# Layer 0's queries of ten token tiles as pairs in seven quadrant products each, with token sums and weight forms made by GpSimd

## The chip, the cores and the metric

The kernel runs on one core of a Trainium2 chip. The metric is device time in microseconds (us) of one execution; the kernel before takes 1817.35 us, the median of three runs (1817.26 to 1817.72). PE is TensorE's matmuls, PEld its weight loads, DVE is VectorE, ACT is ScalarE, POOL is GpSimd, SP is SyncE, which here only issues transfers.

## The reference

Two layers of a graph transformer on 2708 tokens with 512 features, 8 heads of 64, all in float32. Each token attends only to its neighbours (and itself), some 9 on average. Cut to one layer:

```python
mask = adj.astype(jnp.float32) + jnp.eye(n)
q = (h @ Wq.T + bq).reshape(n, 8, 64)
k = (h @ Wk.T + bk).reshape(n, 8, 64)
v = (h @ Wv.T + bv).reshape(n, 8, 64)
scores = jnp.einsum('nhd,mhd->hnm', q, k) / jnp.sqrt(jnp.float32(64))
attn = softmax(jnp.where(mask[None] == 0, -1e9, scores))
ctx = jnp.einsum('hnm,mhd->nhd', attn, v).reshape(n, 512)
h1 = layer_norm(h + ctx @ Wo.T + bo, ln1_g, ln1_b)
ff = relu(h1 @ W1.T + b1) @ W2.T + b2
h2 = layer_norm(h1 + ff, ln2_g, ln2_b)
```

## The kernel before

A token tile is 128 tokens; there are 22 (`NT`), the last of 20 tokens. Layer 0 is run in three stages.

**The keys' pass** (function `first`): for each tile `t`, PE makes its keys and values from the transposed tokens `xg` (four 128x512 matmuls each, L626 in `project`), ACT copies both out of PSUM (L962, L968), POOL adds the keys' bias (L964), and ACT's queue writes the rows to `kv_d`. Tokens are held in three buffers of two tiles each. Beside it, `lists_of` turns the adjacency matrix into lists of neighbours: ACT codes a row block (L746), DVE takes the largest entries (L751 to L758). After the last list, DVE counts (`counted`, L772 to L824: `has`, `count`, `hot`, the running sum `before` and its prefix `run`, L789 to L813), and PE ranks the tokens by their number of neighbours (`ranked`, L834 and L841, matmuls that read `hot` and `before`). These four matmuls stand in PE's queue ahead of the last tile's keys and values (L621) and of every query.

**The queries' pass** (`first_queries`): per tile four 128x512 matmuls against `Wq` (L626), then one DVE instruction that scales, adds the bias and writes to SBUF (`evicted`, L1003). Pairs of tiles are written to `q_d`. After the third tile's product, PE turns the ranking round (`inverted`, L900, 22 small matmuls), DVE makes two index tables of it (L909 to L913), and then `last_keys` (L989 and six times L636) adds up the last tile's keys and values, which it takes from the PSUM places in which they have lain since the keys' pass; their write to `kv_d` is what the first gathers of attention wait for. Between the query tiles stand three "own" queries (L1077) and, from the eighth tile on, steps of attention.

**The blocks**: attention (gathers on POOL's queue, DVE and ACT arithmetic) runs beside out projection and feed forward of eleven blocks of two tiles. From the fifth block on the second feed-forward matrix is multiplied in seven products per quadrant pair instead of eight (`feed_forward_by_seven`, L1769).

The order on every engine is the order in which the program is written (the kernel schedules by hand); each engine runs its queue in order. PSUM has eight places of 128x512: three in the pool `ps_f` (tag "f"), three in `ps` (tag "g"), and two in `ps_a` (`a0`, `a1`). A place is given out again when its last reader is done. In the order of the tiles, keys take "g" and values "f"; query tiles take "g" and "f" in turn.

## Time and profile before

| | |
|---|---|
| runs | 1817.26, 1817.35, 1817.72 us |
| profiled execution, its own time | 1817.08 us |
| span of that execution on the core | 1815.1 us |
| PE busy | 1791.5 us (99%) |
| DVE busy | 1463.3 us (81%) |
| ACT busy | 1001.1 us (55%) |
| POOL busy | 855.4 us (47%) |
| granted TensorE clock | 0.998 |
| keys' pass, first to last matmul | 5.0 to about 154 us |
| queries' pass | 154.3 to about 250 us |

The profile counts each float32 matmul twice, as two passes: 21 full tiles of queries with four matmuls each stand as 168. A matmul's recorded length (592 ns for 512 columns) overlaps the next one's; what counts is the distance from start to start. Engine time in a stretch is read from the windows' view, the order of events from the timeline, whose columns are start, length, engine, line and operation, what is written and read, shape and count.

### The profile page before, as it was taken

What the parts mean: (1) busy time and instruction counts of PE and PEld (TensorE: products, weight loads), DVE (VectorE), ACT (ScalarE), POOL (GpSimd) and SP (SyncE); (2) the same over time, 40 slices, a digit from 0 to 9 for tenths busy, and PEclk for the clock granted to TensorE, in tenths of its full rate; (3) what the DMA queues carried; (4) which work ended last, traced back from release to release, by engine and by line L of the source; (5) the groups of instructions that cost most, each with busy time, mean ns of one, the idle gap of its engine ahead of it and who ended that gap; (6) DMA issues with size and microseconds to landing.
All of it is one profiled execution on the core that took longest, in us unless ns stands there. A gap on an engine that the chain in (4) does not pass through costs nothing. (4 is left out here: it accounts for less than half of the span.)

```text
span 1815.1 us, 23887 instructions
## 1 busy us (share of the span) xinstructions
PE 1791.5 (99%) x6839; PEld 1214.6 (67%) x6839; DVE 1463.3 (81%) x2599; ACT 1001.1 (55%) x3397; POOL 855.4 (47%) x830
## 2 busy tenths in 40 slices
PE   9999999999999999999999999999999999999997
PEld 4444456666777867777677644666666888788786
DVE  4987778988989889799896267988888899989933
ACT  5771436645555555555653104677776677767631
POOL 3333755534454544454540132556665665655312
PEclk9999999999999999999999999999999999999999
DMA  9997987757676675666752777967867787877531
GB/s 335 369 344 252 374 284 245 230 181 241 203 238 220 203 259 192 208 220 202 241 194 73 242 285 272 319 193 256 279 186 263 243 264 237 293 225 234 173 94 36
DMA packets 186728, 426.74 MB, mean 235 GB/s; under 512 B 20550, under 2 KB 83898, under 8 KB 186584
## 3 DMA queue, kind: packets, MB, share of 16 engines
q0 software_dynamic: 76992, 264.49, 44.0%
q1 hardware_dynamic: 99434, 139.01, 22.5%
q10 hardware_dynamic: 10158, 21.61, 3.1%
q8 instruction: 56, 0.92, 0.2%
q14 instruction: 88, 0.72, 0.1%
HBM read 357.13 MB, written 57.11 MB: 228 GB/s over the span
## 5 line engine op out<-in xcount | busy, mean ns | idle before, releaser
L1119 POOL DMA_INDIRECT kv<-kv_d,listed x420 | 526.0, 1252 | 307.2 <-DVE acc L1195 145.8
L1780 PE MATMUL pf<-hT,w 128*128 128x256 f32 x1792 | 407.2, 379 | 2.1 <-ACT ft L1791 2.1
L1780 PEld LDWEIGHTS pf<-hT,w 128*128 128x128 f32 x1792 | 339.2, 190 | 59.2 <-issue 11.0
L1182 ACT ACTIVATE kv<-kv,p 128x64 f32<-128x64 f32 x1232 | 311.0, 335 | 5.0
L1156 DVE TENSOR_TENSOR kv<-kv,q 128x1024 f32<-128x1024 f32 (+1 forms) x222 | 257.1, 1158 | 14.1 <-DMA q<-q_d,ident_i 10.9
L1162 DVE TENSOR_REDUCE sc<-kv 128x16 f32<-128x1024 f32 (+1 forms) x222 | 258.0, 1162 | 7.6
L1195 DVE TENSOR_TENSOR acc<-acc,kv 128x1024 f32<-128x1024 f32 (+2 forms) x178 | 205.6, 1155 | 49.6 <-ACT kv L1182 36.9
L1596 PEld LDWEIGHTS pf<-hT,w 128*128 128x128 f32 x1024 | 178.5, 190 | 55.3 <-issue 34.6
L1596 PE MATMUL pf<-hT,w 128*128 128x256 f32 (+1 forms) x1024 | 214.6, 357 | 0.1
L1791 ACT ACTIVATE ft<-pf,b 128x256 f32<-128x256 f32 x168 | 78.1, 466 | 214.1 <-PE pf L1780 211.4
L1569 PE MATMUL a<-w,ft 128*128 128x512 f32 x416 | 194.6, 592 | 0.0
L1175 ACT ACTIVATE p<-sc,listed 128x8 f32<-128x8 f32 x420 | 103.6, 295 | 127.9 <-DVE sc L1162 116.5
L1281 POOL TENSOR_TENSOR rd<-va,mhalf 128x1 f32<-128x1 f32 (+1 forms) x48 | 43.8, 913 | 230.8 <-DVE va L1279 230.7
L626 PE MATMUL o<-wo,cT 128*128 128x512 f32 x336 | 151.0, 593 | 0.3 <-ACT cT L1354 0.3
L1188 DVE TENSOR_TENSOR kv<-kv,p 128x512 f32<-128x512 f32 (+1 forms) x178 | 123.6, 694 | 4.8 <-ACT p L1175 4.5
L1569 PEld LDWEIGHTS a<-w,ft 128*128 128x128 f32 x416 | 77.7, 190 | 57.5 <-issue 52.0
L626 PEld LDWEIGHTS o<-wo,cT 128*128 128x128 f32 x336 | 63.4, 190 | 69.3 <-issue 59.6
L1331 POOL TENSOR_SCALAR va<-sq 128x1 f32<-128x1 f32 (+1 forms) x40 | 17.2, 429 | 188.4 <-ACT xb L1324 101.9
L751 DVE MAX8 tops<-code 128x8 f32<-128x247 f32 (+2 forms) x242 | 78.8, 400 | 28.0 <-ACT code L746 27.9
L1226 ACT ACTIVATE cx<-acc,su 128x64 f32<-128x64 f32 (+1 forms) x352 | 88.2, 333 | 11.2 <-DVE su L1218 6.2
L1182 ACT ACTIVATE acc<-kv,p 128x64 f32<-128x64 f32 (+1 forms) x352 | 88.8, 335 | 1.4
L746 ACT ACTIVATE code<-aj 128x1354 bf16<-128x1354 int32 (+1 forms) x44 | 73.5, 1724 | 23.7 <-POOL aj L740 19.0
(258 smaller groups left out, 2793.8 us busy)
## 6 DMA issues: line engine op xcount, KB each, us to landing
forms<-form_d SPq DMA_DIRECT2D x294, 128.0 KB, 3.8
aj<-in_adj SPq DMA_DIRECT2D x42, 677.0 KB, 6.3
kv_d<-kvs ACTq DMA_DIRECT2D x21, 512.0 KB, 7.4
h<-ln_b POOLq DMA_DIRECT2D x41, 256.0 KB, 7.0
xg<-in_xT SPq DMA_DIRECT2D x19, 512.0 KB, 8.0
w<-in_W SPq DMA_DIRECT2D x16, 512.0 KB, 6.4
kv<-kv_d,listed POOLq DMA_INDIRECT x420, 6.5
zT_d<-zT SPq DMA_DIRECT2D x22, 256.0 KB, 5.3
```

Of the source, the lines that this page charges most:

```text
L626: nc.tensor.matmul(o[:r], xs(c), wm[:, c, :], start=(c == 0), stop=(c == NC - 1))
L1119: return nc.gpsimd.indirect_dma_start(out=to, out_offset=None, in_=table[:, :], in_offset=bass.IndirectOffsetOnAxis(ap=s, axis=0), bounds_ ...
L1156: nc.vector.tensor_tensor(kv[:r, :c, :DM], kv[:r, :c, :DM], self.q[:r].unsqueeze(1).to_broadcast([r, c, DM]), ALU.mult,)
L1162: nc.vector.tensor_reduce(self.sc[:r, s0 : s0 + c, :], kv[:r, :c, :DM].rearrange("p s (h d) -> p s h d", d=DK), AX.X, ALU.add,)
L1175: nc.scalar.activation(p[:r, s, :], self.sc[:r, s, :], AF.Exp, bias=minus[:r, g, s : s + 1])
L1182: nc.scalar.activation(to[:, i, hd], kv[:r, i, DM + h * DK : DM + (h + 1) * DK], AF.Copy, scale=p[:r, s0 + i, h : h + 1],)
L1188: nc.vector.tensor_tensor(to[:, 0, :].rearrange("p (h d) -> p h d", d=DK), kv[:r, 0, DM:].rearrange("p (h d) -> p h d", d=DK), p[:r, s0, : ...
L1195: nc.vector.tensor_tensor(self.acc[:r, :c, :], self.acc[:r, :c, :], kv[:r, :c, DM:], ALU.add)
L1226: nc.scalar.activation(cx[:r, hd], self.acc[:r, 0, hd], AF.Copy, scale=self.su[:r, h : h + 1])
L1569: nc.tensor.matmul(a[:r, cols], fts[f][:, c0 : c0 + r], self.w2[f // 2][:, f % 2, cols], start=(f == 0), stop=(f == NFC - 1),)
L1596: nc.tensor.matmul(pf[:, :w], self.w1[f // 2][:, c, f % 2 * P : f % 2 * P + P], hT[:, c, :w], start=(c == 0), stop=(c == NC - 1),)
L1780: nc.tensor.matmul(pf[:, :W], self.w1[j][:, c, f % 2 * P : f % 2 * P + P], hT[:, c, :], start=(c == 0), stop=(c == NC - 1),)
```

## The change

Query tiles 0 to 9 of layer 0 are made as five pairs. A pair is a 256x512 matrix of tokens, `Wq` is 512x512; both are cut into four quadrants, and the product is made of seven quadrant products (Winograd's form) instead of eight. Each quadrant product is two matmuls of 128x256, so a pair has 14 of these in place of 8 of 128x512.

- **Token sums.** For each pair POOL makes four combinations of token quadrants (`token_sums`, 128x256 each) in the keys' pass, after tiles 1, 3, 5, 7 and 9, and keeps them in places of `W1` and `W2` that are free until then.
- **Weight forms.** Four combinations of `Wq`'s quadrants (`formed_of`, 128x512 each) and one difference of the bias's halves (`more`, 128x256) are made by POOL in the keys' pass at tile 19.
- **Scale.** 1/8 is put into `Wq` once, by ACT at tile 18 (128x2048); query evictions no longer scale.
- **Products.** At an even tile four of the seven (`first`), at the odd tile three (`second`). A pair needs four PSUM places: pairs 0, 2, 4 take one "f", one "g", `a0` and `a1`; pairs 1 and 3 take two "f" and two "g".
- **Evictions.** Seven DVE instructions per pair (`begun` five, `ended` two) in place of two.
- **Transfers.** In the second pass over the tokens, the first five `xg` loads leave out a quadrant that no product reads, and come as two transfers. Two pairs of feed-forward weight loads move from query tile 10 to 11 (the first of these places holds weight forms until then).

```diff
--- before.py
+++ after.py
@@ -45,6 +45,8 @@
 LEAD = 1.2
 QT = 16
 OWN = 5
+SUMS = ("w1_2", "w1_3", "w2_3", "w1_4", "w2_4")
+FORMQ = ("w2_2", "w1_1")
 WARM = 7
 LISTS = (4, 7, 9, 12, 13, 14, 15, 17, 18, 19)
 EARLY = 3
@@ -636,6 +638,75 @@
                 nc.vector.tensor_tensor(to, part, to, ALU.add)
             else:
                 nc.vector.scalar_tensor_tensor(to, part, scale, to, ALU.mult, ALU.add)
+
+    W2 = 2 * P
+
+    def formed_of(w, to, by):
+
+        b11, b12, b21, b22 = w[:, :2, :W2], w[:, :2, W2:], w[:, 2:, :W2], w[:, 2:, W2:]
+        t1, t2, t3, t4 = to
+        by.tensor_tensor(t3, b22, b12, ALU.subtract)
+        by.tensor_tensor(t1, b12, b11, ALU.subtract)
+        by.tensor_tensor(t2, b22, t1, ALU.subtract)
+        by.tensor_tensor(t4, b21, t2, ALU.subtract)
+
+    def token_sums(a, b, to, by):
+
+        a11, a12, a21, a22 = a[:, :2, :], a[:, 2:, :], b[:, :2, :], b[:, 2:, :]
+        s1, s2, s3, s4 = to
+        by.tensor_tensor(s1, a21, a22, ALU.add)
+        by.tensor_tensor(s2, s1, a11, ALU.subtract)
+        by.tensor_tensor(s3, a11, a21, ALU.subtract)
+        by.tensor_tensor(s4, a12, s2, ALU.subtract)
+
+    class Seven:
+
+
+        def __init__(self, a, b, sums, w, forms, banks):
+            s1, s2, s3, s4 = sums
+            t1, t2, t3, t4 = forms
+            L, R = slice(0, W2), slice(W2, DM)
+            self.c0, self.c1, self.a0, self.a1 = banks
+            self.first = (
+                (self.c0[:, L], a[:, :2, :], w[:, :2, L]),
+                (self.c0[:, R], s2, t2),
+                (self.c1[:, L], s1, t1),
+                (self.c1[:, R], s3, t3),
+            )
+            self.second = (
+                (self.a0[:, L], a[:, 2:, :], w[:, 2:, L]),
+                (self.a0[:, R], s4, w[:, 2:, R]),
+                (self.a1[:, L], b[:, 2:, :], t4),
+            )
+
+        def products(self, which):
+            for to, left, right in which:
+                for c in range(2):
+                    nc.tensor.matmul(
+                        to, left[:, c, :], right[:, c, :], start=(c == 0), stop=(c == 1)
+                    )
+
+        def begun(self, q, bias, more, wide=None):
+
+            L, R = slice(0, W2), slice(W2, DM)
+            nc.vector.tensor_tensor(q[0], self.c0[:, L], bias[:, L], ALU.add)
+            nc.vector.tensor_tensor(q[3], self.c0[:, R], q[0], ALU.add)
+            nc.vector.tensor_tensor(self.c1[:, L], self.c1[:, L], more, ALU.add)
+            if wide is None:
+                nc.vector.tensor_tensor(q[2], self.c1[:, R], q[3], ALU.add)
+                nc.vector.tensor_tensor(q[1], self.c1[:, L], q[3], ALU.add)
+            else:
+                nc.vector.tensor_tensor(
+                    wide.rearrange("p (two n) -> p two n", two=2),
+                    self.c1.rearrange("p (two n) -> p two n", two=2),
+                    q[3].unsqueeze(1).to_broadcast([P, 2, W2]),
+                    ALU.add,
+                )
+            nc.vector.tensor_tensor(q[3], self.c1[:, L], q[2], ALU.add)
+
+        def ended(self, first, q2):
+            nc.vector.tensor_tensor(first, self.a0, first, ALU.add)
+            nc.vector.tensor_tensor(q2, self.a1[:, :W2], q2, ALU.add)
 
     def finish(steps):
         for _ in steps:
@@ -925,6 +996,12 @@
             t = wts.tile([P, NC, XB], F32, tag=f"w1_{5 + i % 3}", name="xg")
             xg.append(t)
             step = bw if i else P
+            if i >= XBS and i % XBS < len(SUMS):
+                src = chunked(xT)
+                nc.sync.dma_start(out=t[:, :2, :P], in_=src[:, :2, b : b + P])
+                nc.sync.dma_start(out=t[:, 2:, :], in_=src[:, 2:, b : b + bw])
+                yield
+                return
             for a in range(0, bw, step):
                 (by if a else nc.sync).dma_start(
                     out=t[:, :, a : a + step], in_=chunked(xT)[:, :, b + a : b + a + step]
@@ -950,7 +1027,7 @@
         wv = matrix(w, "Wv", "wv")
         pa = tc.tile_pool(name="pa", bufs=2)
         lists, counted, placing = lists_of(pa.__enter__())
-        done, before = 0, None
+        done, before, sums = 0, None, []
         for t in range(NT):
             r = size(t)
             if t == NT - 1:
@@ -980,10 +1057,23 @@
                 bk = row_of(short[0], "bk")
                 nc.gpsimd.tensor_tensor(kv[:r, :DM], kv[:r, :DM], bk[:r], ALU.add)
             meanwhile(t)
+            if t % 2 and t // 2 < len(SUMS):
+                place = wts.tile([P, 4, 2, P], F32, tag=SUMS[t // 2], name="sums")
+                x2 = xg[t // 2]
+                sums.append([place[:, i] for i in range(4)])
+                token_sums(x2[:, :, :P], x2[:, :, P:], sums[-1], nc.gpsimd)
             if t == QT:
                 wq = matrix(w, "Wq", "wq", nc.gpsimd)
+            if t == QT + 2:
+                nc.scalar.activation(wq, wq, AF.Copy, scale=DK**-0.5)
             if t == NT - 4:
                 bq = row_of(short[1], "bq", DK**-0.5)
+            if t == NT - 3:
+                forms = [wts.tile([P, 2, 2, W2], F32, tag=tag, name="forms") for tag in FORMQ]
+                forms = [place[:, i] for place in forms for i in range(2)]
+                formed_of(wq, forms, nc.gpsimd)
+                more = dn.tile([P, W2], F32, tag="hT", name="more", bufs=1)
+                nc.gpsimd.tensor_tensor(more, bq[:, W2:], bq[:, :W2], ALU.subtract)
 
         def last_keys():
             nc.vector.tensor_tensor(kv[:r, :DM], k[:r], bk[:r], ALU.add)
@@ -991,19 +1081,19 @@
             plus_rest(kv[:r, DM:], v, r)
             nc.scalar.dma_start(**before)
 
-        return bq, wq, parts, placing[1], pa, tokens, last_keys
-
-    def first_queries(bq, wq, parts, inverted, pa, tokens, last_keys, meanwhile):
+        sevens = xg, sums, forms, more
+        return bq, wq, sevens, parts, placing[1], pa, tokens, last_keys
+
+    def first_queries(bq, wq, sevens, parts, inverted, pa, tokens, last_keys, meanwhile):
 
         nonlocal at
+        xg, sums, forms, more = sevens
         made = []
 
         def evicted(t, q, qs):
             r = size(t)
-            nc.vector.scalar_tensor_tensor(
-                qs[:r, t % 2], q[:r], DK**-0.5, bq[:r], ALU.mult, ALU.add
-            )
-            plus_rest(qs[:r, t % 2], q, r, DK**-0.5)
+            nc.vector.tensor_tensor(qs[:r, t % 2], q[:r], bq[:r], ALU.add)
+            plus_rest(qs[:r, t % 2], q, r)
 
         def written():
             t, qs = made.pop(0)
@@ -1017,7 +1107,25 @@
 
         for t in range(NT):
             r = size(t)
-            q = project(tokens(t, 1), r, wq, "q", other=t % 2 > 0)
+            xs = tokens(t, 1)
+            seven = t // 2 < len(sums)
+            if not seven:
+                q = project(xs, r, wq, "q", other=t % 2 > 0)
+            elif t % 2 == 0:
+                x2 = xg[t // 2 + XBS]
+                banks = [ps_f.tile([P, DM], F32, tag="f", name="q0")]
+                banks.append(ps.tile([P, DM], F32, tag="g", name="q1"))
+                if t % 4:
+                    banks.append(ps_f.tile([P, DM], F32, tag="f", name="q2"))
+                    banks.append(ps.tile([P, DM], F32, tag="g", name="q3"))
+                else:
+                    banks += [
+                        ps_a.tile([P, DM], F32, tag=f"a{i}", name=f"q{2 + i}") for i in range(2)
+                    ]
+                q = Seven(x2[:, :, :P], x2[:, :, P:], sums[t // 2], wq, forms, banks)
+                q.products(q.first)
+            else:
+                q.products(q.second)
             if t % 2 == 0 and made:
                 written()
             if t == 2:
@@ -1036,7 +1144,15 @@
             if t % 2 == 0:
                 qs = wts.tile([P, 2, DM], F32, tag=f"w2_{5 + (t // 2 + 1) % 3}", name="qs")
                 made.append((t, qs))
-            evicted(t, q, qs)
+            if not seven:
+                evicted(t, q, qs)
+            else:
+                flat = qs.rearrange("p two n -> p (two n)")
+                quarters = [flat[:, i * W2 : (i + 1) * W2] for i in range(4)]
+                if t % 2 == 0:
+                    q.begun(quarters, bq, more, flat[:, W2 : 3 * W2])
+                else:
+                    q.ended(flat[:, :DM], quarters[2])
             if t in LISTS:
                 i = 2 + 2 * LISTS.index(t)
                 for g in order[i : i + 2]:
@@ -1074,8 +1190,8 @@
 
         r = size(g)
         q = project(lambda c: zT[:, c, :r], r, wq, "q")
-        nc.vector.scalar_tensor_tensor(to[:r], q[:r], DK**-0.5, bq[:r], ALU.mult, ALU.add)
-        plus_rest(to[:r], q, r, DK**-0.5)
+        nc.vector.tensor_tensor(to[:r], q[:r], bq[:r], ALU.add)
+        plus_rest(to[:r], q, r)
 
     def put(table, s, rows, group):
 
@@ -1996,9 +2112,9 @@
 
     def beside_queries(t):
 
-        if t in (8, 10, 12, 14):
-            now.load_w1(t // 2 - 4, nc.gpsimd)
-            now.load_w2(t // 2 - 4, nc.gpsimd)
+        if t in (8, 11, 12, 14):
+            now.load_w1(len(now.w1), nc.gpsimd)
+            now.load_w2(len(now.w2), nc.gpsimd)
         if t == 6:
             now.settle()
         if t == 16:
```

Names in the rows below: `q`, with its numbers, is a PSUM place of a query; `forms` and `sums` are the weight forms and token sums; `kvs` are a tile's keys and values on their way to `kv_d`.

On PE, at the head of the queries' pass, the kernel before has:

```order
L834 MATMUL pr<-hot,tri 128x264
L841 MATMUL pr<-before,ones 128x264
L621 MATMUL k<-wk,xg 20x512 x4
L621 MATMUL v<-wv,xg 20x512 x4
L626 MATMUL q<-wq,xg 128x512 x12
```

and the changed one, pair 0 and the first half of pair 1:

```order
L905 MATMUL pr<-hot,tri 128x264
L912 MATMUL pr<-before,ones 128x264
L623 MATMUL k<-wk,xg 20x512 x4
L623 MATMUL v<-wv,xg 20x512 x4
L685 MATMUL q_1269<-wq,xg 128x256 x2
L685 MATMUL q_1269<-forms,sums 128x256 x2
L685 MATMUL q_1270<-forms,sums 128x256 x4
L685 MATMUL q_1271<-wq,xg 128x256 x2
L685 MATMUL q_1271<-wq,sums 128x256 x2
L685 MATMUL q_1272<-forms,xg 128x256 x2
L685 MATMUL q_1298<-wq,xg 128x256 x2
```

Twelve matmuls of 512 columns (three tiles) ahead of L900 have become 22 of 256 columns (a pair and four products of the next). Behind L900 the changed PE goes on with the second half of pair 1 and then pair 2:

```order
L685 MATMUL q_1300<-wq,xg 128x256 x2
L685 MATMUL q_1300<-wq,sums 128x256 x2
L685 MATMUL q_1301<-forms,xg 128x256 x2
L685 MATMUL q_1417<-wq,xg 128x256 x2
L685 MATMUL q_1417<-forms,sums 128x256 x2
L685 MATMUL q_1418<-forms,sums 128x256 x4
```

With the waits shown, the first matmul into `q_1417` waits for DVE, and the one into `q_1300` does not:

```order
L685 MATMUL q2_1300<-wq_1037,xg_1195 128x256 [waits DMAHW1_49]
L685 MATMUL q2_1300<-wq_1037,xg_1195 128x256
L685 MATMUL q2_1300<-wq_1037,sums_375 128x256 x2
L685 MATMUL q3_1301<-forms_1188,xg_1195 128x256 x2
L685 MATMUL q0_1417<-wq_1037,xg_1266 128x256 [waits DMAHW1_49,DVE_49,Activation_49]
```

`q_1300` and `q_1301` are pair 0's first two places; `q_1417` and `q_1418` are the places of the last tile's values and keys, whose last reader is the last L638 of `last_keys`.

On POOL, at the end of the keys' pass, before:

```order
L964 TENSOR_TENSOR kvs<-kvs,bk 128x512
L613 TENSOR_SCALAR bq<-bq 128x512
L964 TENSOR_TENSOR kvs<-kvs,bk 128x512
L576 DMA wo<-in_Wo 128x512 x4
L964 TENSOR_TENSOR kvs<-kvs,bk 128x512
```

and changed:

```order
L1041 TENSOR_TENSOR kvs<-kvs,bk 128x512
L615 TENSOR_SCALAR bq<-bq 128x512
L1041 TENSOR_TENSOR kvs<-kvs,bk 128x512
L578 DMA wo<-in_Wo 128x512 x4
L648 TENSOR_TENSOR forms<-wq 128x512
L649 TENSOR_TENSOR forms<-wq 128x512
L650 TENSOR_TENSOR forms<-wq,forms 128x512
L651 TENSOR_TENSOR forms<-wq,forms 128x512
L1076 TENSOR_TENSOR more<-bq 128x256
L1041 TENSOR_TENSOR kvs<-kvs,bk 128x512
```

Five instructions stand between the issue of `Wo` and the bias of tile 20's keys.

On DVE, around `inverted` and `last_keys`, before:

```order
L1003 SCALAR_TENSOR_TENSOR qs<-q,bq 128x512 x2
L909 COPY sums<-to 128x44
L910 TENSOR_TENSOR ident_i<-sums 128x22
L911 TENSOR_SCALAR sums<-sums 128x22
L912 TENSOR_SCALAR sums<-sums 128x22
L913 TENSOR_TENSOR place_i<-sums 128x22
L989 TENSOR_TENSOR kvs<-k,bk 20x512
L636 TENSOR_TENSOR kvs<-k,kvs 20x512 x3
L636 TENSOR_TENSOR kvs<-v,kvs 20x512 x3
```

and changed, pair 0 ahead of it and the begin of pair 1 behind it:

```order
L708 TENSOR_TENSOR qs<-q_1271,qs 128x512
L709 TENSOR_TENSOR qs<-q_1272,qs 128x256
L980 COPY sums<-to 128x44
L981 TENSOR_TENSOR ident_i<-sums 128x22
L982 TENSOR_SCALAR sums<-sums 128x22
L983 TENSOR_SCALAR sums<-sums 128x22
L984 TENSOR_TENSOR place_i<-sums 128x22
L1079 TENSOR_TENSOR kvs<-k,bk 20x512
L638 TENSOR_TENSOR kvs<-k,kvs 20x512 x3
L638 TENSOR_TENSOR kvs<-v,kvs 20x512 x3
L2027 MEMSET peak 128x22
L692 TENSOR_TENSOR qs<-q_1298,bq 128x256
```

The order there is kept; the two evictions ahead of L909 have become the seven of pair 0.

## The prediction

> **What bounds the kernel now.** I read the page's engine shares first (PE 99%), then the windows of the first 250 us, then the timeline of PE, DVE and POOL from 139 to 215 us, and last the groups by line for the prices.
>
> The windows (PE, PEld, DVE, ACT, POOL busy, clock, DMA):
>
> ```profile
> 0.00:100.00 100.00, 98.33 (x235) 45.17 (x236) 72.13 (x264) 64.62 (x59) 33.14 (x63) 1.00 0.96 356
> 195.00:210.00 15.00, 15.00 (x39) 6.85 (x38) 13.60 (x20) 8.99 (x37) 11.75 (x12) 1.00 1.03 392
> ```
>
> PE is full in both passes at full clock; in the queries' pass DVE is nearly full too. So a microsecond off PE's queue comes off the end, and one in which PE waits is added, as long as no other queue decides. PE at the seam of the two passes:
>
> ```profile
> 150.60 0.61 PE L834 MATMUL pr<-hot,tri 128*128 128x264 f32 x2
> 151.04 0.61 PE L841 MATMUL pr<-before,ones 128*128 128x264 f32 x2
> 154.32 10.57 PE L626 MATMUL q<-wq,xg 128*128 128x512 f32 x24
> 164.72 0.81 PE L900 MATMUL to<-table 128*128 128x44 bf16 x22
> 165.46 10.57 PE L626 MATMUL q<-wq,xg 128*128 128x512 f32 x24
> ```
>
> No gap. But L841 reads `before`, and DVE makes that at the last moment:
>
> ```profile
> 142.42 1.65 DVE L777 TENSOR_TENSOR hot<-count,by 128x528 f32<-128x528 f32 x1
> ...
> 144.15 2.39 DVE L789 TENSOR_TENSOR before<-before,hot 128x48 f32<-128x48 f32 x10
> ...
> 147.81 0.17 DVE L808 COPY run<-run 128x2 f32<-128x2 f32 x1
> ...
> 148.10 1.28 DVE L808 COPY run<-run 128x4 f32<-128x4 f32 x1
> ...
> 150.05 0.71 DVE L813 TENSOR_TENSOR before<-before,run 128x528 f32<-128x528 f32 x1
> ```
>
> L813 ends at 150.76; PE takes it at 151.04. The margin is at most 0.28 us, and behind L841 stand in PE's queue the last tile's keys and values and all queries. Two of these rows are too long: L777 takes 1.65 for a shape that L813 does in 0.71, and the COPY at 148.10 takes 1.28 where the one before it took 0.17. Both stand beside a POOL addition:
>
> ```profile
> 142.24 1.25 POOL L964 TENSOR_TENSOR kvs<-kvs,bk 128x512 f32<-128x512 f32 x1
> 143.44 2.22 POOL L576 DMA_DIRECT2D wo<-in_Wo  x4
> 148.09 1.26 POOL L964 TENSOR_TENSOR kvs<-kvs,bk 128x512 f32<-128x512 f32 x1 [2.43 <-issue]
> ```
>
> The COPY came 0.01 us after its POOL instruction and lost 1.11 of 1.26 us; L777 came 0.18 after and lost 0.94 of 1.25. POOL itself lost nothing.
>
> **The change, part by part.** *PE's saving.* From a later stage, distances from start to start:
>
> ```profile
> 600.45 3.60 PE L626 MATMUL o<-wo,cT 128*128 128x512 f32 x8
> 603.88 1.89 PE L1780 MATMUL pf<-hT,w 128*128 128x256 f32 x8
> 605.61 0.59 PE L1769 MATMUL a<-forms,ft 128*128 128x256 f32 x2
> ...
> 608.63 3.62 PE L1780 MATMUL pf<-hT,w 128*128 128x256 f32 x16
> ```
>
> Eight passes of 512 columns take 3.43 us (600.45 to 603.88), so a float32 matmul of 512, two passes, takes 0.857. From 605.61 to 608.63 stand seven matmuls of 256: 0.431 each, weight loads hidden. A pair took 8 x 0.857 = 6.86 us and will take 14 x 0.431 = 6.04; five pairs save 5 x 0.82 = **4.1 us**.
>
> *POOL's sums and forms.* Prices:
>
> ```profile
> L964 POOL TENSOR_TENSOR kvs<-kvs,bk 128x512 f32<-128x512 f32 x20 | 25.4, 1270 | 50.7 <-ACT kvs L962 39.8 <-issue 4.8 <-DMA aj<-in_adj 3.9
> L740 POOL TENSOR_TENSOR aj<-aj,diag 128x128 int32<-128x128 int32 x20 | 8.7, 432 | 29.1 <-DMA aj<-in_adj 29.1
> ```
>
> On the line through both, 128x256 takes 0.71 us: four token sums 2.85, four forms 5.08, `more` 0.71. The sums follow an L740 and have the hole up to the next tile's bias:
>
> ```profile
> 40.89 0.45 POOL L740 TENSOR_TENSOR aj<-aj,diag 128x128 int32<-128x128 int32 x1
> 45.21 1.27 POOL L964 TENSOR_TENSOR kvs<-kvs,bk 128x512 f32<-128x512 f32 x1 [3.86 <-ACT kvs L962]
> ```
>
> 3.86 us hold 2.85. Beside them DVE searches for neighbours, and that is as long with a POOL addition beside it (108.27) as without one (135.73):
>
> ```profile
> 107.14 3.56 DVE L751 MAX8 tops<-code 128x8 f32<-128x247 f32 x11
> ...
> 135.73 3.55 DVE L751 MAX8 tops<-code 20x8 f32<-20x247 f32 x11
> ```
> ```profile
> 108.27 1.27 POOL L964 TENSOR_TENSOR kvs<-kvs,bk 128x512 f32<-128x512 f32 x1 [2.34 <-ACT kvs L962]
> ```
>
> Cost nothing. Without that hole a pair's sums would put the next bias off by 2.85 us, and the write of those keys behind it; PE waits for neither.
>
> The forms are another matter. They start when `Wo`'s issue ends, at 143.44 + 2.22 = 145.66, and five instructions of 5.79 us lie right on DVE's chain from L789 to L813, most of whose instructions are TENSOR_TENSOR and COPY, as the two that lost time are. The bias addition that costs 1.11 already comes behind them and costs the same again. Bounds of what DVE loses: nothing, if small DVE instructions slip in and the forms wait; all 5.79, if nothing overlaps. DVE always has its next instruction ready, as the COPY at 148.10 had, so I take that row's share, 1.11/1.26 = 0.88: 5.1 us. Less PE's margin (0 to 0.28), **PE waits 4.9 us at L841** (bounds 0 and 5.8). A gain is excluded: nothing of the chain is taken away.
>
> The Trainium skill's page "SBUF — State Buffer" (section "Who interferes with whom") has the rule: a DVE instruction with two SBUF inputs, or a copy in a two-port mode, and a GpSimd instruction that reads SBUF exclude each other for a whole instruction, and whoever comes first blocks the other. The trace agrees (1.11 lost of 1.26). By the rule to the letter DVE loses all 5.79, PE waits 5.6, and the total below would be 0.7 higher.
>
> *Scale of `Wq` on ACT.*
>
> ```profile
> L746 ACT ACTIVATE code<-aj 128x1354 bf16<-128x1354 int32 (+1 forms) x44 | 73.5, 1724 | 23.7 <-POOL aj L740 19.0
> ```
> ```profile
> 137.07 0.59 ACT L968 COPY kvs<-v 128x512 f32<-128x512 f32 x1 [1.91 <-PE v L626]
> 140.50 0.59 ACT L962 COPY kvs<-k 128x512 f32<-128x512 f32 x1 [2.85 <-DMA kv_d<-kvs]
> ```
>
> 128x2048 at L746's rate is 1.72 x 2048/1354 = 2.6 us, in a hole of 2.85. Hidden, and done before 145.66; uncovered it delays one copy, and three PSUM places of keys hide that.
>
> *Evictions.* Prices per instruction, and DVE's work around `last_keys`:
>
> ```profile
> L1003 DVE SCALAR_TENSOR_TENSOR qs<-q,bq 128x512 f32<-128x512 f32 x21 | 14.2, 683 | 11.1 <-PE q L626 9.4 <-DMA kv_d<-kvs 1.7
> L1825 DVE TENSOR_TENSOR u<-c,u 128x512 f32<-128x512 f32 x14 | 9.7, 692 | 1.5
> L1824 DVE TENSOR_TENSOR u<-c,u 128x256 f32<-128x256 f32 x14 | 5.9, 425 | 1.5
> ```
> ```profile
> 159.00 1.62 DVE L884 TENSOR_TENSOR table<-lane,lanes 128x1408 bf16<-128x1408 f32 x1
> 165.57 0.20 DVE L909 COPY sums<-to 128x44 f32<-128x44 f32 x1 [3.38 <-PE to L900]
> ...
> 166.41 0.67 DVE L989 TENSOR_TENSOR kvs<-k,bk 20x512 f32<-20x512 f32 x1
> 167.12 2.13 DVE L636 TENSOR_TENSOR kvs<-k,kvs 20x512 f32<-20x512 f32 x3
> 169.27 2.13 DVE L636 TENSOR_TENSOR kvs<-v,kvs 20x512 f32<-20x512 f32 x3
> ```
>
> A pair costs DVE 5 x 0.425 + 2 x 0.692 = 3.5 us instead of 2 x 0.683 = 1.4: 2.1 more, 10.5 in all. Now the seam without the wait at L841, on the old clock. PE: pair 0 from 154.32, 6.04, to 160.36; four products of pair 1 (8 x 0.431) to 163.8. L900 needs `a0`, which pair 0 used: DVE is free of L884 at 160.6, and six of the seven evictions (4 x 0.425 + 2 x 0.692 = 3.1) bring it to 163.7. That fits. L900 goes from 163.8 to 164.55 (0.74, as before from 164.72 to 165.46), 0.9 earlier than before; so DVE's tables and `last_keys` also come 0.9 earlier and end at 171.40 - 0.9 = 170.5. PE makes three products of pair 1 in the places of pair 0 (2.59) until 167.15, and then pair 2 needs the two places in which the last tile's keys and values lie: free at 170.5. **PE waits 3.4 us there**, 3.5 with DVE's lost margin. Before, tiles 4 and 5 took the places of tiles 0 and 1 and nothing waited. Bounds: 3.3, since every length on this way is that of a row which stays; 4.1, if one more DVE instruction (0.7) must end before L900 can start, which holds PE there by as much. Behind the wait stand pair 2 and the own queries; DVE then has two pairs to evict (7.0 us) and catches up while PE makes pair 2 and two own queries (6.04 + 6.9).
>
> *The rest of DVE's load.* From the ninth tile on DVE is nearly full, and 2.1 us late per pair:
>
> ```profile
> 207.54 0.64 DVE L1003 SCALAR_TENSOR_TENSOR qs<-q,bq 128x512 f32<-128x512 f32 x1
> 208.69 0.69 DVE L1077 SCALAR_TENSOR_TENSOR q<-q,bq 128x512 f32<-128x512 f32 x1 [0.51 <-PE q L626]
> 212.12 0.69 DVE L1003 SCALAR_TENSOR_TENSOR qs<-q,bq 128x512 f32<-128x512 f32 x1 [2.74 <-PE q L626]
> ```
>
> Only pair 4 and the end of pair 3 fall into the full stretch (some 2.5 us), and 0.51 + 2.74 us of waiting for PE take it up; nothing. Without those, up to 2.5 us.
>
> *Transfers.* Five more issues on SP, for fewer bytes; each load still goes out when its buffer falls free. The weight loads moved on POOL's queue pass behind two gathers; their first use is behind the whole pass. Nothing.
>
> **Sum:** 1817.08 - 4.1 + 4.9 + 3.5 = 1821.4 in terms of the profiled execution, which is 0.27 under the median of the runs: **1821.6 us**, slower by 0.24%.
>
> **Rivals.** *A, the forms cost DVE nothing.* For it: only two DVE instructions were seen to lose time, and the chain's small ones may slip in; against it: both lost nearly the whole POOL instruction. Then -4.1 + 3.4 = -0.7: 1816.7. Halfway, a loss of 2.5 at L841, gives +1.8: 1819.2. *B, a clear gain:* both waits hidden. One mechanism would do it, DVE done with `last_keys` 3.4 us earlier and with `before` on time; the rows show no such reserve. -4.1: 1813.2. *C, DVE becomes the bound after tile 8:* the 10.5 us of evictions push the first attention steps, PE waits for their context before the out projections; it decides once DVE's lateness exceeds the 3.25 us of waiting above. All of the 2.5 us on top: 1824.1. Against it: after PE's two waits DVE has more slack, not less.
>
> **How the numbers follow.** Forecast 0.57 (own range 1820.4 to 1822.7), A with its halfway house 0.27, C 0.10, B 0.06. A measurement of this kernel tells about 0.2% from no change: faster is below 1813.7, slower above 1821.0. The forecast lies above that in about 0.7 of its share (0.40), C whole (0.10): slower 0.50. B is faster, with a little of A: 0.07. The rest, 0.43, is no change. The range reaches from A to the upper end of the forecast and the edge of C: 1816.4 to 1823.0.
>
> **What would show it.** Right: a PE gap of 4 to 5.5 us in front of L912 (released by DVE's prefix sum), L648 to L651 back to back beside stretched DVE rows; a second gap of about 3.5 us in front of pair 2, released by L638; seven products every 6.04 us; no gaps in the keys' pass from the sums. Wrong: the chain ending near 150.8 as before (A), or PE gaps at the out projections near 220 us (C). A time under 1815 would mean that both waits are elsewhere hidden and my reading of the seam is false.

## The result, and the profile after

The changed kernel takes **1842.40 us**, the median of four runs (1842.13 to 1843.67), against 1817.37 for the kernel before in the same comparison: ratio 1.0139, 95% interval 1.0121 to 1.0156. The forecast was 1821.6 and a range up to 1823.0. The direction is right, the size is not: 25.0 us more instead of 4.3. The profiled execution took 1842.24 us with a span of 1840.5 (before: 1817.08 and 1815.1), so the trace holds all of the difference.

The windows of the changed kernel (columns as in the prediction: length, PE, PEld, DVE, ACT, POOL busy, granted clock, DMA share, GB/s):

```profile
0.00:100.00 100.00, 96.85 (x232) 43.97 (x233) 59.18 (x217) 51.28 (x48) 43.06 (x75) 1.00 0.80 295
100.00:150.00 50.00, 47.00 (x106) 20.38 (x105) 45.61 (x167) 40.92 (x36) 16.52 (x31) 0.97 0.98 371
150.00:200.00 50.00, 34.36 (x148) 23.33 (x147) 43.44 (x98) 4.54 (x7) 21.79 (x23) 0.83 0.58 190
200.00:250.00 50.00, 49.85 (x160) 28.20 (x159) 39.73 (x61) 22.60 (x88) 37.83 (x36) 1.00 0.99 355
```

The damage is done before 200 us, and the first sign of it is not on PE. In the first 100 us DVE works 59.18 us instead of 72.13 and the DMA engines move 295 GB/s instead of 356: the search for neighbours runs late because its transfers come late. Between 150 and 200 PE is busy 34.36 of 50 us, and its clock, which was 1.00 throughout, is granted at 0.83.

PE around the seam of the passes, to be read beside the rows of the prediction (L905 and L912 are the old L834 and L841, L685 the new products):

```profile
156.72 0.61 PE L905 MATMUL pr<-hot,tri 128*128 128x264 f32 x2
169.77 1.25 PE L912 MATMUL pr<-before,ones 128*128 128x264 f32 x2 [12.43 <-DVE before L884]
...
175.71 1.13 PE L685 MATMUL q<-wq,xg 128*128 128x256 f32 x4
...
187.88 1.03 PE L685 MATMUL q<-forms,xg 128*128 128x256 f32 x4
192.12 1.99 PE L685 MATMUL q<-wq,xg 128*128 128x256 f32 x4 [3.21 <-issue]
...
199.92 1.04 PE L1465 MATMUL tp<-ident,xr 128*128 128x128 f32 x8
```

```profile
223.59 0.60 PE L1465 MATMUL tp<-ident,xr 128*128 128x128 f32 x4
```

The second `tp` row stood at 201.18 in the kernel before:

```profile
201.18 0.60 PE L1349 MATMUL tp<-ident,xr 128*128 128x128 f32 x4
```

Subtracting the old start of each row gives a bill of the difference:

| up to | before | after | lateness | added in this step |
|---|---|---|---|---|
| L905, end of the keys' pass | 150.60 | 156.72 | 6.1 | 6.1: PE waits in the keys' pass |
| L912 | 151.04 | 169.77 | 18.7 | 12.6: the wait for `before` |
| first query | 154.32 | 175.71 | 21.4 | 2.7: the matmuls behind that wait are slow |
| `tp`, after three pairs | 175.86 | 199.92 | 24.1 | 2.7: the second wait, 3.2 to 3.4, slow matmuls behind it, 1.8, less three pairs' saving, 2.5 |
| `tp`, after five pairs | 201.18 | 223.59 | 22.4 | -1.65: two pairs' saving |
| end of the span | 1815.1 | 1840.5 | 25.4 | 3.0, in small steps at many places |

The last 3.0 us are not told apart: the kernel before spreads over 1815 to 1823 us on other chips in the same comparisons.

**Where the first 6.1 and half of the 12.6 come from.** The waits of SP's own queue between 15 and 150 us (engine and line, what it waited for, sum, times, longest), after and before:

```profile
SPq L1006 <- POOL sums L660: 56.1, 5, 13.2
SPq L808 <- ACT code L817: 32.8, 20, 2.3
```

```profile
SPq L737 <- ACT code L746: 59.2, 35, 3.7
SPq L929 <- PE v L626: 30.1, 8, 8.3
```

L1006 (before: L929) is the load of the next two tiles' tokens into one of three buffers. It used to wait for PE, the only reader of the buffer. Now POOL reads it too, for the token sums, and SP waits for the last of them. Behind this load in SP's queue stand the loads of the adjacency matrix (L808), and on these wait POOL's diagonal, then ACT's codes, then DVE's searches. The first round of it, on POOL, SP, POOL again and ACT:

```profile
29.53 0.73 POOL L660 TENSOR_TENSOR sums<-xg,sums 128x256 f32<-128x256 f32 x1
...
37.81 0.46 POOL L811 TENSOR_TENSOR aj<-aj,diag 128x128 int32<-128x128 int32 x1 [4.75 <-DMA aj<-in_adj]
```

```profile
30.28 0.38 SPq L1006 DMA_DIRECT2D xg<-in_xT  x1
30.77 2.73 SPq L808 DMA_DIRECT2D aj<-in_adj  x4
```

```profile
38.30 1.73 ACT L817 ACTIVATE code<-aj 128x1354 bf16<-128x1354 int32 x1 [6.24 <-POOL aj L811]
```

In the kernel before SP sent this load at 20.33:

```profile
20.33 0.52 SPq L929 DMA_DIRECT2D xg<-in_xT  x1
```

Ten microseconds later, then, and right behind the end of L660 (29.53 + 0.73 = 30.26). The adjacency loads behind it go at 30.77 instead of 27.65, and in the next round at 47.29 instead of 37.05: the lateness has grown from 3.1 us to 10.2. ACT, whose copies of keys stand in its queue between the codes, comes late with these too, and that is what PE waits for in the keys' pass:

```profile
113.82 5.30 PE L628 MATMUL k<-wk,xg 128*128 128x512 f32 x8 [2.32 <-ACT kvs L1039]
```

There are four such waits, 4.4 us in all; the other 1.7 of the 6.1 are slow matmuls behind this one, the longest.

**The rest of the 12.6** is the counting on DVE. Its first instruction starts at 153.52 (before: L772 at 140.80), 12.7 us late; from there to the end of L884 it takes 16.2 us (before: 10.0), 6.2 us longer. One group of ten small additions has grown by more than that; the two rows that a POOL addition had stretched before (old L777 and the COPY at 148.10) are now 0.94 and 1.11 shorter:

```profile
140.80 0.84 DVE L772 TENSOR_SCALAR has<-top 128x528 f32<-128x528 f32 x1
```

```profile
153.52 0.85 DVE L843 TENSOR_SCALAR has<-top 128x528 f32<-128x528 f32 x1
...
155.95 10.66 DVE L860 TENSOR_TENSOR before<-before,hot 128x48 f32<-128x48 f32 x10
...
169.00 0.71 DVE L884 TENSOR_TENSOR before<-before,run 128x528 f32<-128x528 f32 x1
```

```profile
156.03 1.27 POOL L1041 TENSOR_TENSOR kvs<-kvs,bk 128x512 f32<-128x512 f32 x1 [1.04 <-ACT kvs L1039]
157.24 2.22 POOL L578 DMA_DIRECT2D wo<-in_Wo  x4
159.47 1.27 POOL L648 TENSOR_TENSOR forms<-wq 128x512 f32<-128x512 f32 x1
...
165.28 1.27 POOL L1041 TENSOR_TENSOR kvs<-kvs,bk 128x512 f32<-128x512 f32 x1
```

The ten took 2.39 us before and take 10.66 now, 8.27 more. POOL's arithmetic beside them is 1.27 at 156.03 and 7.08 from 159.47 to 166.55, 8.35 in all: DVE lost 0.99 of it.

### The profile page after: what moved, and what is told of

Read it like the earlier page. It is cut to its first block, busy times and chain, and to the rows that moved or that the text cites. A ratio compares the mean times of both kernels' runs of the same rounds, so it can differ in the third digit from the quotient of the medians.

```text
span 1840.5 us, 24066 instructions
## 1 busy us (share of the span) xinstructions
PE 1795.4 (98%) x6899; PEld 1228.2 (67%) x6899; DVE 1479.6 (80%) x2624; ACT 1003.3 (55%) x3398; POOL 876.5 (48%) x855
## 4 chain that ended last, share of the span: by engine, by line
PE 70%; DVE 10%; DMA 6%; issue 6%; ACT 4%; POOL 3%; SPq 0%; ACTq 0%; POOLq 0%; DVEq 0%
PE pf L1896 16%; PE pf L1712 8%; PE c L1885 7%; PE a L1685 7%; PE o L628 7%; PE a L1885 5%; PE k L628 4%; PE v L628 4%; PE q L628 4%; PE tp L1465 2%; DMA aj<-in_adj 2%; DVE kv L1272 2%; DVE sc L1278 2%; PE q L685 1%; ACT code L817 1%
```

## The experiments

Each run is compared with the kernel before on its own chip, and the ratios below are to that. Where it is said how late PE is at a row, the profiled execution of the kernel before is the zero.

**1. The token sums ahead of the searches.** In the changed kernel the block of `token_sums` moves to the start of the odd tile:

```diff
             xs = tokens(t, 0)
+            if t % 2 and t // 2 < len(SUMS):
+                ...
+                token_sums(x2[:, :, :P], x2[:, :, P:], sums[-1], nc.gpsimd)
...
             meanwhile(t)
-            if t % 2 and t // 2 < len(SUMS):
-                ...
```

> Edit: in the changed kernel, the token sums of a pair are issued on POOL at the start of the odd tile, ahead of its bias addition and of that tile's searches, instead of behind them. Nothing else is changed. Theory H (held buffer): in the changed kernel SP's loads of the tokens waited 56.1 us in five waits for POOL's last token sum (L660, longest 13.2), where before they waited for PE alone; adjacency loads stand behind them on SP, so ACT, DVE's searches and the counting came 12.7 us late. With the sums ahead of the adjacency additions the loads go out as before, the last search ends near 141 us as before, and only the forms' 6.2 us on DVE's counting chain, the wait ahead of pair 2 and the slow matmuls after each of these two PE waits (some 2 us each) are left: 1817.4 - 4.1 + 5.9 + 2 + 3.4 + 1.8 = about 1826 us. Rival W (work): five times 2.9 us of POOL, or what they take from DVE, delay the searches wherever they stand: still about 1840 us.

Measured: 1834.71 us against 1819.90 on this chip, ratio 1.0080 (1.0063 to 1.0097). That is between the two theories. SP's waits say why:

```profile
SPq L808 <- ACT code L817: 51.0, 30, 2.9
SPq L1006 <- POOL sums L660: 25.0, 5, 7.3
```

The wait for the sums is halved, not gone, and the counting starts at 143.89, 3.1 us late instead of 12.7. The first sums now stood behind POOL's wait for the keys' bias row (to 22.94 us) and ended at 27.07, and SP's load went at 27.09 instead of 20.33.

**2. The token sums alone.** The kernel before, with the sums added at the place where the change has them and read by nobody:

```diff
             meanwhile(t)
+            if t % 2 and t // 2 < len(SUMS):
+                place = wts.tile([P, 4, 2, P], F32, tag=SUMS[t // 2], name="sums")
+                ...
+                token_sums(x2[:, :, :P], x2[:, :, P:], sums[-1], nc.gpsimd)
```

> Edit: the kernel before with the five pairs' token sums alone added on POOL, at the place where the change has them; nobody reads them, and queries are made as before. Theory H: the whole lateness of the searches comes from these sums by way of SP: keys' pass about 6 us longer, the counting 12.7 us late, and slow matmuls after a PE wait of some 6 us: 1817.4 + 12.4 + 2 = about 1832 us. Rival: the lateness needs the change's other parts (split token loads, scale of Wq): then about 1817 to 1820 us.

Measured: 1834.20 us, ratio 1.0080 (1.0063 to 1.0097), some 14.5 us (11.5 to 17.7). SP waited 55.5 us for L660, the counting started at 153.17, and the queries began 14.6 us late (168.94). So instructions whose results are thrown away, on an engine that was a third busy, cost 14.5 us, and the change's other parts aren't needed for it. Whether they cost it as readers of a buffer or by POOL's time, this run alone can't say; the fifth does.

**3. The forms alone.** The kernel before, with `formed_of` and `more` added at the change's place, read by nobody:

```diff
                 bq = row_of(short[1], "bq", DK**-0.5)
+            if t == NT - 3:
+                ...
+                formed_of(wq, forms, nc.gpsimd)
+                ...
+                nc.gpsimd.tensor_tensor(more, bq[:, W2:], bq[:, :W2], ALU.subtract)
```

> Edit: the kernel before with the four forms and `more` alone added on POOL, at the place where the change has them (from an unscaled Wq); nobody reads them. In the changed kernel the ten small additions at L860 took 10.66 us instead of 2.39 beside them. Theory P (the port is shared whole): the counting chain grows by the forms' full time, 5.8 to 6.2 us, PE waits that long at the prefix sums, and matmuls behind the wait run slowly for some us (+2): about 1825 us. By the prediction's share of 0.88 and no slow matmuls: 1822.3 us. If the forms cost DVE nothing (the prediction's rival A): 1817.4 us.

Measured: 1827.69 us, ratio 1.0047 (1.0030 to 1.0064). PE around the wait (L863 is the old L841):

```profile
156.08 1.25 PE L863 MATMUL pr<-before,ones 128*128 128x264 f32 x2 [5.55 <-DVE before L835]
157.12 1.09 PE L856 MATMUL pr<-hot,tri 128*128 128x264 f32 x2
...
159.02 1.45 PE L623 MATMUL k<-wk,xg 128*20 128x512 f32 x8
```

A wait of 5.55 us, as the prediction's bounds had it (0 to 5.8), but the time is 5.5 to 11.6 us above before, where the prediction's numbers gave 4.9 (the 1822.3 is for a chip on which before takes 1817.4; here it takes 1819.9). PE leaves the wait 5.04 us late and begins the queries 6.95 us late (161.26 against 154.32).

**4. Other PSUM places for the third pair.** As the first run, with

```diff
+                    pairs = other + pairs if t else pairs + other
```

(`other` are `a0` and `a1`, `pairs` are f and g): the third and fifth pairs begin in `a0` and `a1`, so that the third doesn't need the two places of the last tile's keys and values at once.

> Edit: as the run with the sums ahead, and the third and fifth pairs put their first four products in the places a0 and a1 and their last three in f and g, instead of the other way round, so that the third pair doesn't begin in the two places where the last tile's keys and values wait for DVE. Theory B: the wait of 3.2 to 3.4 us ahead of the third pair goes, and with it the 1.8 us of slow matmuls behind it: 5 us below the run with the sums ahead, about 1821 us. Rival: another release (a0 read by DVE behind the tables, or DVE's evictions) takes its place, and the time is as with the sums ahead, about 1826 us.

Measured: 1829.88 us, ratio 1.0058 (1.0042 to 1.0075). In the first run the third pair's first product came behind a wait, and the sixteen matmuls from there took 5.1 us instead of 3.45:

```profile
181.88 2.05 PE L685 MATMUL q<-wq,xg 128*128 128x256 f32 x4 [3.21 <-issue]
183.72 3.42 PE L685 MATMUL q<-forms,sums 128*128 128x256 f32 x12
186.98 1.03 PE L685 MATMUL q<-wq,xg 128*128 128x256 f32 x4
```

With the other places it has no wait, and PE is 8.3 us late at `tp` instead of 13.7: 5.4 us, 0.4 of which it was already ahead at the first query (165.08 against 165.48), the rest the wait and the slow matmuls together. In time the run is 4.8 us below the first by the medians, with intervals that overlap. Theory B holds, by the trace.

**5. The sums first of all.** As the fourth run; the first pair's sums go ahead of the keys' bias row, the others to the start of the even tile:

```diff
+            if t % 2 == 0 and 0 < t // 2 < len(SUMS):
+                summed(t // 2)
...
             if t == 0:
+                summed(0)
                 bk = row_of(short[0], "bk")
```

> Edit: as the run with the other places for the third and fifth pairs, and the token sums still earlier on POOL: those of the first pair ahead of the wait for the keys' bias row, those of a later pair at the start of its even tile. With the sums at the odd tile the first of them ended at 27.07 us (20.33 is when SP sent that load before), SP still waited 25.0 us for sums, and the last search ended 3.1 us late (143.89 against 140.80). Theory H: now SP waits for PE alone again, the searches end within 0.5 us of before, and of the PE wait at the prefix sums (8.6 us in the run with the sums ahead) the forms' 5.5 to 6 us are left: 3 us less than the run before it with these places (1829.9 us on its chip, where before had 1819.9): before + 7. Rival: the remaining 3.1 us come from POOL's work of 14.5 us itself, and the time stays at before + 10.

Measured: 1826.09 us, ratio 1.0040 (1.0024 to 1.0055), some 7.3 us. SP no longer waits for POOL at all:

```profile
SPq L808 <- ACT code L817: 58.3, 34, 3.8
SPq L1006 <- PE v L628: 18.6, 5, 8.5
```

The counting starts 0.8 us earlier than before, with the same twenty additions on POOL:

```profile
139.99 0.85 DVE L843 TENSOR_SCALAR has<-top 128x528 f32<-128x528 f32 x1
```

So it was the held buffer and not the work: theory H, whole. PE's wait at the prefix sums is 5.5 us, the forms' share.

**6. The forms early.** As the fifth run; `Wq` is loaded at tile 10 instead of 16, the queries' bias with it, and one form is made per tile beside the searches:

```diff
-QT = 16
+QT = 10
...
-                formed_of(wq, forms, nc.gpsimd)
+                forming = formed_of(wq, forms, nc.gpsimd)
...
+            if QT + 3 <= t < QT + 7:
+                next(forming)
```

> Edit: as the run with the sums first, and Wq and the queries' bias loaded six to eight tiles earlier, Wq scaled three tiles behind that, and the forms made one per tile beside the searches (MAX8), which POOL's additions have not lengthened in any trace, instead of all four beside the counting. Theory P: nothing of POOL but one bias addition is left beside the counting chain, no PE wait over 3 us and so no slow matmuls are left anywhere in the first 250 us, and the saving of the products, 4.1 us, shows: before - 4, faster than before by 0.2%. Rival D (DMA): the transfers of Wq, 2.5 us of all sixteen engines, now stand among the adjacency's, whose DMA share is 0.9 to 1.0 there, and the searches end up to 2.5 us later: before - 4 + 2.5 (+2 of slow matmuls if the PE wait gets past some 3 us), that is before - 1.5 to before + 0.5.

Measured: 1817.76 us, ratio 0.9996 (0.9987 to 1.0005): the 25 us are gone, but the saving does not show. In the trace it is there at first. PE is 4.45 us early at `tp` (201.18 before), the whole 4.1 and 0.7 by which it was already ahead at the first query (153.61 against 154.32), less some small losses; at 290 us it is 0.5 us early.

```profile
196.73 0.60 PE L1478 MATMUL tp<-ident,xr 128*128 128x128 f32 x4
```

In between stand these waits of PE, all that exceed 0.2 us from 150 to 300 us:

```profile
PE pf L1725 <- ACT ft L1736: 2.4, 2, 1.4
PE tp L1478 <- DVE qs L1104: 0.7, 1, 0.7
```

Rival D's time would fit (before - 1.5 to before + 0.5), but its mechanism does not: the counting starts at 140.59, no later than before and 0.6 us later than in the fifth run, so the earlier load of `Wq` cost the searches at most that. Something behind the queries holds the gain back; three more pairs of runs looked for it.

**7. The wait filled.** The third run's kernel, with L858, the first product of the prefix sums, made thirteen times instead of once:

```diff
+                n = 1 if h else 13
+                for i in range(n):
...
+                        stop=i < n - 1,
```

> Edit: the run with the forms alone, and the first product of the prefix sums repeated twelve times more ahead of L863 (same operands, same place, each starting anew; some 5.3 us of TensorE), in the PE wait of 5.5 us. Theory C (clock): matmuls behind a PE wait of over some 3 us run at half speed for 3 to 6 us, whatever the wait's cause; in the run with the forms alone PE came out of the wait 5.04 us late and began the queries 6.95 us late, so 1.9 us are the slow matmuls'. Filled, the wait's end stays where it is and the 1.9 us go: queries begin 5.0 to 5.3 us late, the time is 1.9 us below that of the forms alone. Rival: the matmuls behind the wait are slow for another reason (operands that DVE and POOL write or read beside them): still 6.9 us.

Measured: 1825.05 us, ratio 1.0039 (1.0026 to 1.0051); its interval and the third run's overlap, so the time doesn't tell the two apart. The trace does:

```profile
150.04 5.95 PE L858 MATMUL pr<-hot,tri 128*128 128x264 f32 x26
156.20 0.71 PE L865 MATMUL pr<-before,ones 128*128 128x264 f32 x2 [0.21 <-DVE before L835]
...
157.73 1.06 PE L623 MATMUL k<-wk,xg 128*20 128x512 f32 x8
```

PE still gets `before` 5.15 us late, but nothing is slow behind it: L865 takes 0.71 instead of 1.25, the queries begin 5.25 us late (159.57) instead of 6.95. Useless work in a wait took 1.7 us off PE's lateness, so the waiting itself had cost them, and not the operands of the matmuls behind it.

**8. Less work for PE alone.** The kernel before, with five query tiles made from three of four chunks (their values are incomplete):

```diff
+            n = NC - 1 if t in (0, 2, 4, 6, 8) else NC
+            q = project(tokens(t, 1), r, wq, "q", other=t % 2 > 0, n=n)
```

> Edit: the kernel before, with the queries of tiles 0, 2, 4, 6 and 8 made from three of the four chunks of 128 columns: five products of 512 columns fewer (5 x 0.857 = 4.3 us of TensorE, the same as the five pairs of seven products save), and nothing else on any engine. These queries are incomplete, so their values are not the reference's. In the run with the forms early PE was 4.45 us ahead of before at 196.7 us, 3.5 at 245 and 0.47 at 290: it waited there for ACT's `ft` behind the attention steps, which began at 263.21 us instead of 263.66. Theory B (bound): PE is full in the queries' pass but doesn't decide its end alone; the first attention steps on DVE, POOL's gathers, and the last evicted queries stand in an order of their own, and the gain is kept back there although no eviction is longer: before - 0.5 to before - 1. Rival E (evictions): the 10.5 us of longer evictions on DVE ate it, and without them the whole gain comes off the end: before - 4.

Measured: 1816.83 us, against 1820.55 on this chip; ratio 0.9980 (0.9972 to 0.9989), 2.0 to 5.1 us. Theory B, that only 0.5 to 1 us of it would show, falls; the time fits rival E, with the whole gain, as well as a part of it. In the trace PE is 4.6 us early at `tp` and 2.3 at 290, so half is kept back by then, though no eviction is longer. That the evictions kept back the sixth run's gain isn't shown by this; the tenth run, which has them too, speaks against it.

**9. The last queries evicted first.** As the sixth run, with the last attention step moved behind the last evictions:

```diff
-        if t > OWN + 1:
+        if OWN + 1 < t < NT - 3:
             advance(0.65)
+        if t == NT - 1:
+            advance(1.5)
```

> Edit: the run with the forms early, with the last attention step on DVE ahead of the last evicted queries (3.2 us, L1285 to L1324, 245.2 to 248.4 us) moved behind them, so that the queries' last tiles are evicted, written and gathered earlier. Theory Q: DVE's wait of 11.3 us for the gathered queries (263.21 us) starts from the last eviction (251.86 us), which stood behind attention steps; it ends 2.5 to 3 us earlier, PE's waits for `ft` (2.4 us) go, and 2 to 3 us of the saving come off the end: before - 2 to before - 3.5. Rival: the step that was moved is itself on the path behind the gather (it has to be done before the next one), or POOL's gathers hold it: no change from the run with the forms early (before + 0.1).

Measured: 1820.09 us, against 1820.55; ratio 0.9996 (0.9987 to 1.0004), the same as the sixth. The last eviction ended 1.7 us earlier (250.1 instead of 251.8), POOL issued the gather of queries 0.6 us earlier (256.94 instead of 257.57), and the attention behind it still began at 263.17 (263.21 in the sixth, 263.66 before). Theory Q falls.

**10 and 11. POOL's weight loads on ACT's queue**, in the sixth run's kernel and in the kernel before:

```diff
-            now.load_w1(len(now.w1), nc.gpsimd)
-            now.load_w2(len(now.w2), nc.gpsimd)
+            now.load_w1(len(now.w1), nc.scalar)
+            now.load_w2(len(now.w2), nc.scalar)
```

> Edit: the run with the forms early, with the eight weight loads that POOL issues among its gathers in the queries' pass (L1509, L1516, 0.74 to 0.84 us each, 6.4 us in all) issued by ACT instead. In all runs POOL's gathers follow each other from the first one (166.78 us before, 165.28 with the forms early) to 254 us with 0.30 us between them, and end within a microsecond of each other whatever PE does (253.05, 252.30, and 252.07 with less work for PE). Theory G: POOL's chain of gathers, not PE, sets when the attention steps, and with them the first gathered queries (q<-q_d, 258.18 before, 257.57 with the forms early) can come; 6.4 us shorter, it lets 3 to 4 us of the saving through: before - 2.5 to before - 4. Rival M: the gathers themselves wait for the DMA engines (share 1.04 there), so that POOL's time is only moved: no change from the run with the forms early (before - 0.7 on its interval of -2.4 to +0.9).

> Edit: the kernel before with the same eight weight loads issued by ACT instead of POOL; nothing else. In the kernel before PE has no gap in this pass, so it is the bound there, with POOL's gathers hardly behind. Theory G: relieving POOL alone gives nothing while PE is full: before, within 1 us. Rival: POOL alone is the bound in the kernel before too: before - 2 to before - 4.

Measured: 1818.62 us, ratio 1.0001 (0.9992 to 1.0010), and 1819.26, ratio 1.0007 (0.9998 to 1.0016), both against 1818.19. In time neither gains, and theory G's forecast of 2.5 to 4 us for the tenth is missed. In the trace the tenth does what theory G said, up to a point. PE's waits for `ft` are gone; from 196 to 300 us this is all that is left:

```profile
PE tp L1478 <- ACT cx L1355: 0.2, 1, 0.2
```

PE is 4.4 us early at 196.81 and still 4.1 at 506.67 (before: 510.76), where the sixth run is only 0.4 early. So it was POOL's queue, with the load issues among its gathers, that held back the sixth run's saving there; the evictions are as long in both runs. Then, in the second layer, PE waits for tokens that are streamed through three buffers (1080 to 1130 us of the tenth run):

```profile
PE q L628 <- DMA zT<-zT_d: 2.6, 2, 2.3
```

Against the eleventh run's trace, the 4.4 us of lead have become 2.7 behind this wait and 2.0 at 1577 us. That the end has less than that, 0.6 us between the medians, is within what these runs can tell. No version that makes all queries whole beats the kernel before by more than its measurement is uncertain.

## Why the prediction was right or wrong, step by step

**PE's saving: right.** A pair takes 6.04 us where nothing interferes, as forecast:

```profile
214.12 1.03 PE L685 MATMUL q<-wq,xg 128*128 128x256 f32 x4
...
220.16 3.60 PE L628 MATMUL q<-wq,xg 128*128 128x512 f32 x8
```

**"Cost nothing" for the token sums: the step that failed.** The prediction asked whether POOL has time for them (3.86 us for 2.85; a sum takes 0.73 us, 0.71 was forecast) and whether they slow DVE (they don't: the rows at the end of this document), and both answers were right. It did not ask whose buffer they read. The part on transfers says that "each load still goes out when its buffer falls free", without the next question: who frees it now. The sums stood behind an adjacency addition, that addition waits for a transfer, and what waits for the sums stands ahead of the next such transfers. The prediction even named "no gaps in the keys' pass from the sums" as a sign that it would be right; the trace has four such gaps there. Runs 2 and 5 price it: 14.5 us when the sums alone are there, nothing when they read early. In the changed kernel it is 6.1 us in the keys' pass and 6.4 of the 12.6 at L912 (12.7 of late counting less those 6.1, less PE's margin), 12.5 of the 20.8 us by which the forecast was too low.

**The forms beside the counting: the right mechanism, sized low.** 4.9 was forecast; the counting became 6.2 longer, and the wait of the forms alone is 5.55. The share that DVE loses is 0.99 instead of the 0.88 taken from one row, for the forms and for the two bias additions beside the counting, which had cost 0.94 and 1.11 before. The Trainium skill's rule in "SBUF — State Buffer" (section "Who interferes with whom"), by the letter, gave 5.6 for the wait: here the rule was better than the row, which was one COPY that had come 0.01 us late. Rival A is out.

**The wait ahead of the third pair: right.** 3.5 forecast; 3.21 as the profile has it, 3.4 from start to start, in the place named, with the last L638 ending at 192.02 and the products starting at 192.12. It was avoidable by the order of two places (run 4).

**PE's waits were costed at their length: wrong, and a term is missing.** Matmuls behind some of them run at half speed: 2.7 us behind the first wait, 1.8 behind the second, and 1.7 inside the 6.1 of the keys' pass (the eight of 113.82 take 5.14 to the next row's 118.96 instead of 3.43). Together 6.2 us, nearly a third of the forecast's error; the 1.7 are also among the 12.5 of the sums. The sum of the prediction had no term for it, nor had any rival.

**"A microsecond off PE's queue comes off the end": mostly, and not with what the change adds.** Run 8 takes 4.3 us off PE and gains 2.0 to 5.1. The sixth run takes 4.1 off, with the evictions on DVE and the changed order on POOL, and lies between 2.4 below before and 0.9 above. The prediction's rival C looked for this on DVE after tile 8; run 10's trace puts nearly all of what is lost up to 500 us on POOL, whose gathers follow each other 0.3 us apart. How much of what comes off there reaches the end was not settled, nor was what the gather of queries waits for after the last eviction (run 9).

**Evictions, scale of `Wq`, transfers on POOL's queue: not seen** in the changed kernel's trace as a wait of PE. That the two waits left DVE slack for them is likely, but not shown. In the sixth run, without those waits, PE waits 0.7 us for an eviction near 244 us; in run 8, whose evictions are not longer, it waits 0.6 at the same place.

## What to carry to other kernels

An instruction that reads a shared buffer becomes one of those who free it. Before an added reader is costed at nothing, name the transfer that refills the buffer, the queue in which it stands, what stands behind it there, and what the new reader itself waits for; if that leads back to the same queue, the cost is a round trip per refill and not the instruction's time. And price a PE wait as its length plus the slow matmuls that may stand behind it: 1.7 to 2.7 us here behind waits of 2.3 us and more, with one such wait that cost nothing more.

## What the runs showed of the hardware

**TensorE can pay for a wait twice.** Five windows of the changed kernel and of the tenth run, the granted clock third from the end:

```profile
169.00:176.00 7.00, 6.23 (x23) 2.65 (x24) 6.28 (x18) 0.14 (x1) 0.00 (x0) 0.56 0.19 78
192.00:196.00 4.00, 3.88 (x10) 3.18 (x11) 3.47 (x10) 0.00 (x0) 1.72 (x3) 0.57 0.65 214
...
115.00:117.00 2.00, 2.00 (x4) 0.84 (x3) 1.86 (x9) 1.51 (x2) 0.67 (x3) 0.50 1.02 418
117.00:119.00 2.00, 2.00 (x6) 0.80 (x5) 1.97 (x8) 2.00 (x4) 0.34 (x1) 0.98 1.02 419
```

```profile
1116.00:1120.00 4.00, 4.00 (x13) 1.91 (x12) 0.59 (x1) 1.66 (x8) 0.00 (x0) 1.00 0.35 131
```

After waits of 12.43, 5.55 and 3.21 us the matmuls ran at about half speed for 3 to 6 us (behind the 5.55, in the third run, the clock was granted at 0.50 from 156 to 158 us and at 1.00 from 160). After 2.32 us at 113.82 they did too; after 2.33 us at 1115.70 in the tenth run they did not. The Trainium skill's page "TensorE: Matmul & The Clock Gate" (section "What's actually happening") has the clock halved after an idle window of some 3.4 us and restored after as long a busy one. The two longest waits, the recovery, and the cure in run 7 agree with it; the 3.21 us, and the 2.32 that were enough once, are shorter than such a window, and no run here explains them.

**Two engines exclude each other for whole instructions, down to the smallest.** Ten DVE additions of 0.24 us lost 8.27 of the 8.35 us that POOL added beside them; one of the ten took 207 ns at the least, 1182 in the median and 1878 at the most, as if most of them waited for a whole POOL instruction. MAX8 lost nothing: 401 ns each in the keys' pass before, and 401 with the token sums beside them (groups by line and form, 10 to 140 us, before and after; the idle time ahead of them is the late transfers).

```profile
L751 DVE MAX8 tops<-code 128x8 f32<-128x247 f32 x210 | 68.8, 401 | 28.0 <-ACT code L746 27.9
```

```profile
L822 DVE MAX8 tops<-code 128x8 f32<-128x247 f32 x196 | 64.2, 401 | 40.6 <-ACT code L817 40.6
```
